# One 512-column v product per chunk for half of the heads, an in-place normalisation, and one distance tile for each large block

## The chip, the cores and the metric

The kernel is one program on one core of one Trainium2 chip. It is written in Bass with the Tile layer: the author writes operations on tiles, and a list scheduler fixes, before the kernel runs, the order of the instructions on each engine and the semaphores between them. The metric is the device time of one execution in microseconds (us). The kernel before takes 4754.6 us, the median of three runs (4753.3 to 4758.81).

The engines are TensorE (PE: matmuls; PEld: its weight loads), VectorE (DVE), ScalarE (ACT), GpSimd (POOL) and SyncE (SP), which issues nearly all DMAs. Everything is float32.

## The reference

Eight sequences of 512 tokens with 128 features pass through two blocks. The first is a causal attention with 16 heads of 8 features whose weights come from four Newton steps on lam, with weights 1/(lam - s). The second is a stack of six layers, each with a local attention (16 heads of 64 features, windows of 32 tokens) and a gated feed-forward part.

```python
x = x + attn(layernorm(x), Wqkv, Wo)            # first part: 16 heads of 8, Newton for lam
z = layernorm(x)
for i in range(6):                               # second part
    z = attn_layer(shift_tokens(z), Wqkv[i], q_scale[i], k_scale[i], Wo[i]) + z
    z = ffn_layer(shift_tokens(z), ln_g[i], ln_b[i], W1[i], b1[i], W2[i], b2[i]) + z
x = x + z

def attn_layer(x, Wqkv, qs, ksc, Wo):
    q, k, v = heads(x @ Wqkv)                    # 16 heads of 64
    q, k = rotary(l2norm(q) * qs), rotary(l2norm(k) * ksc)
    return local_attention(q, k, v) @ Wo         # each window of 32 sees itself and the one before
```

The change touches how v is made in `attn_layer`, and, in the first part, the layer norm and the tile that holds the distances lam - s of a block of queries.

## The kernel before

Two streams of work share the engines.

The first part (`streams`, L168 to L498) is a generator that is advanced in small steps. `project` (L203) loads one sequence into `xb`, `normalized_T` (L177) writes the normalised copy into a second tile `xn` on POOL (L189 to L194), PE transposes it, and ACT writes the transpose back (L199); q, k and v of the first part come from it. `evaluations` (L294) runs the Newton steps. For the two large blocks of queries, rb 3 and rb 2, it takes a distance tile `d` (L298) from a pool of two buffers, both as wide as block 3 needs (1856 columns), and block 2 uses the first 1344 of them. `enter` (L510) calls `normalized_T` again for the input of the second part.

The second part is a loop (L971 to L1045). A unit is one layer of one sequence; there are 48. A unit has four quarters of four heads, and a quarter has two pairs of heads, so a unit takes eight passes of the loop, and there are 384 passes. In each pass the program text asks, in this order, for: `turn` (L738, transposes of q and k, product tiles `ptq`, copies `qT`), `gather` (L790, the sums over the keys, from `v3`), `turn_weights` (L782, `pT`), `prepare_qk` of a half of a later quarter (L670: two products `m` of 512 columns, each multiplied by the tables on DVE at L683 and squared on ACT at L689, with two additions on POOL), `turn_sums` (L812: transposes `po` of L815 and the copy `oT`, L819), `weigh` (L752, 32 x 2 small score products `s`), `prepare_v` (L710), one step of the feed-forward part of the unit before (`further`, L943), and `leave` (L821: the output product `acc`, which reads `oT`). Between these, `tick` advances the first part. The first part has no steps left from about 3480 us on, and from there the passes are the second part alone.

A quarter is prepared over two passes: in each, `prepare_qk` and `prepare_v` treat two of the four chunks of 128 tokens. `prepare_v` makes, for the four heads of the quarter, one product of 256 columns for each of the two chunks; both go into one PSUM bank, and one ACT copy of 128x512 (L718) takes them to the staging tile `v`, of which there are three in rotation (L655, L668). A float32 product is issued to PE as two weight loads and two matmul instructions. After the second pass of a quarter `spread` (L723) issues 18 DMAs on SP that lay v out by windows in `v3`.

The feed-forward part of a unit begins in the pass after the unit's last one, and one of its steps stands in each pass between `prepare_v` and `leave`: its transposes, then the gate products `gp` (three), then the value products `ap` (three), then the products `y` (three).

Most product tiles of the second part come from one pool, `ps_a`, of three PSUM banks (`bank`, L646; its other branch is not reached with eight sequences, since `done_steps` ends at 29 x 72 and the branch asks for 33 x 72). A product has to wait until the last reader of its bank is done. In the passes looked at, the scheduler gave `prepare_v` the bank of the pass's first product `m`.

Of the kernel before, what the change touches and what calls it, by code (L numbers as in the profile page):

```python
# [9 lines left out]
F32 = mybir.dt.float32  # L10
# [6 lines left out]
P = 128  # L17
N = 512
NT = N // P
D = 128  # L20
# [9 lines left out]
DHL = 64  # L30
# [20 lines left out]
def tile_kernel(  # L51
# [18 lines left out]
    nc = tc.nc  # L70
# [22 lines left out]
    dp = ctx.enter_context(tc.tile_pool(name="dp", bufs=2))  # L93
    tr = ctx.enter_context(tc.tile_pool(name="tr", bufs=1))
    pj = ctx.enter_context(tc.tile_pool(name="pj", bufs=1))
# [72 lines left out]
    def streams(pools, bank1):  # L168

        ns_p, dp, tr, pj, sm = pools  # L170
# [6 lines left out]
        def normalized_T(xb, dst):  # L177
            st = sm.tile([P, NT, 6], F32, name="st")
            mv = sm.tile([P, NT, 2], F32, name="mv")
            for c in range(NT):  # L180
                nc.vector.bn_stats(st[:, c, :], xb[:, c, :])
                nc.vector.bn_aggr(mv[:, c, :], st[:, c, :])
                if c % 2:
                    yield
            rstd = sm.tile([P, NT], F32, name="rstd")
            nc.scalar.activation(rstd, mv[:, :, 1], AF.Ln, bias=eps_ln)
            nc.scalar.activation(rstd, rstd, AF.Exp, scale=-0.5)
            yield
            xn = pj.tile([P, NT, D], F32, name="xn", tag="xn")  # L189
            for c in range(NT):  # L190
                nc.gpsimd.tensor_scalar(
                    xn[:, c, :], xb[:, c, :], mv[:, c, 0:1], rstd[:, c : c + 1],
                    ALU.subtract, ALU.mult,
                )  # L194
                yield
            pt = bank1([P, N], "pt")
            for c in range(NT):
                nc.tensor.transpose(pt[:, c * P : (c + 1) * P], xn[:, c, :], ident)
            nc.scalar.copy(dst if dst is not None else xn.rearrange("p c d -> p (c d)"), pt)  # L199
            yield  # L200
            return xn.rearrange("p c d -> p (c d)")
# [30 lines left out]
        def keys(rb, a):  # L232
            return (rb + 1) * P - Q * (3 - a)

        def pieces(d, rb):
            at = [sum(keys(rb, c) for c in range(a)) for a in range(5)]
            return [d[:, at[a] : at[a + 1]] for a in range(4)]

        def width(rb):
            return sum(keys(rb, a) for a in range(4))  # L240
# [44 lines left out]
        def halves(d, rb):  # L285
            n = keys(rb, 0) + keys(rb, 1)
            return d[:, 0:n], d[:, n : width(rb)]

        def statistics(t, d, rb, a):
            nc.vector.bn_stats(  # L290
                t["st"][:, 4 * rb + a].rearrange("p u k -> p (u k)"), pieces(d, rb)[a]
            )

        def evaluations(t):  # L294

            late = []
            for rb in (3, 2):
                d = dp.tile([P, width(3)], F32, name="d")[:, 0 : width(rb)]  # L298
                for h in range(2):
                    for a in (2 * h, 2 * h + 1):  # L300
                        c = 4 * rb + a
                        nc.scalar.activation(  # L302
                            pieces(d, rb)[a], pieces(t["ns"][rb], rb)[a], AF.Ln,
                            bias=t["lam"][:, c : c + 1],
                        )
                    if late:
                        statistics(t, *late.pop(0))
                    yield
                    e = halves(d, rb)[h]
                    nc.scalar.activation(e, e, AF.Exp, scale=-1.0)  # L310
                    if late:
                        statistics(t, *late.pop(0))
                    yield
                    late += [(d, rb, 2 * h), (d, rb, 2 * h + 1)]
            for rb in (1, 0):
                d = t["df"][rb]
                nc.scalar.activation(d, d, AF.Ln)
                if late:
                    statistics(t, *late.pop(0))
                if rb:  # L320
                    yield
                nc.scalar.activation(d, d, AF.Exp, scale=-1.0)
                if late:
                    statistics(t, *late.pop(0))
                yield
                late += [(d, rb, a) for a in range(4)]
            for n in (3, 3, 2):
                for _ in range(n):
                    if late:
                        statistics(t, *late.pop(0))  # L330
                yield
# [87 lines left out]
        def stieltjes(seqs):  # L419
# [36 lines left out]
            def newton(now, k):  # L456
                if k == 0:
                    first_lam(now)
                    yield
                now["st"] = sm.tile([P, H, 2, 3], F32, name="stw")  # L460
                now["df"] = {}
                for rb in (1, 0):
                    now["df"][rb] = d = dp.tile([P, width(rb)], F32, name=f"df{rb}", bufs=1)
                    add_lam(now, d, rb)
                yield
                yield from evaluations(now)
                step(now)
                yield
# [107 lines left out]
    k2 = ctx.enter_context(tc.tile_pool(name="k2", bufs=1))  # L576
# [69 lines left out]
    def bank(shape, name):  # L646
        if done_steps >= (4 * NB + 1) * STEPS:
            turns["n"] += 1
            if turns["n"] % 5 > 2:
                return ps_1.tile(shape, F32, name=name, tag="p1")  # L650
        return ps_a.tile(shape, F32, name=name, tag="mm")

    PQ = 2
    HQ = 2 * PQ
    vst = [k2.tile([P, NT, 2, PQ, DHL + 1], F32, name=f"v{i}") for i in range(3)]  # L655
    for v in vst:
        nc.gpsimd.memset(v.rearrange("p c e h d -> p (c e h) d")[:, :, DHL:], 1.0)

    guarded = [k2.tile([P, 2, 2 * HQ, 2], F32, name=f"raw{i}") for i in range(3)]
    for raw in guarded:  # L660
# [4 lines left out]
    def begin(u, qt, xs):  # L665
        qn = qp.tile([P, NT, 2, HQ, DHL], F32, name="qn")
        v3 = vp.tile([P, NQ, PQ, DHL + 1], F32, name="v3")
        return dict(u=u, qt=qt, xs=xs, qn=qn, v3=v3, v=vst[len(groups) % 3])  # L668

    def prepare_qk(g, wqkv, tab, cs):  # L670
        xs, q0 = g["xs"], (g["qt"] % 2) * HQ * DHL
# [36 lines left out]
            )  # L708

    def prepare_v(g, wqkv, cs):  # L710
        xs, q0 = g["xs"], (g["qt"] % 2) * PQ * DHL
        pv = bank([P, 2, 2, PQ * DHL], "pv2")
        cols = wqkv[:, 2, :].rearrange("i (e f) -> i e f", e=2)[:, :, q0 : q0 + PQ * DHL]
        for i, c in enumerate(cs):
            nc.tensor.matmul(  # L715
                pv[:, i], lhsT=xs[:, c * P : (c + 1) * P], rhs=cols, start=True, stop=True,
            )
        nc.scalar.copy(  # L718
            g["v"][:, cs[0] : cs[0] + 2].rearrange("p c e h d -> p (c e h) d")[:, :, 0:DHL],
            pv.rearrange("p c e (h d) -> p (c e h) d", d=DHL),  # L720
        )

    def spread(g):  # L723
        v3 = g["v3"].rearrange("p n h d -> p n (h d)")
        vc = g["v"].rearrange("p c e h d -> p c e (h d)")
        for e in range(2):
            at = slice(e * KB, e * KB + WIN)
            for u in range(UB):
                own = vc[u * QB : (u + 1) * QB, :, e]
                c = 1 if u == 0 else 0  # L730
                nc.sync.dma_start(v3[e * KB + WIN : (e + 1) * KB, u + c * UB :: UB, :], own[:, c:])
                if u < UB - 1:
                    nc.sync.dma_start(v3[at, u + 1 :: UB, :], own)
                else:
                    nc.sync.dma_start(v3[at, UB::UB, :], own[:, 0 : NT - 1])
            nc.sync.dma_start(v3[e * KB : (e + 1) * KB, 0, :], vc[0:KB, 0, e])
# [183 lines left out]
    groups = []  # L920
# [25 lines left out]
    def open_quarter(i):  # L946
        u, qt = quarters[i]
        if qt == 0 and units[u][0] == 0:
            settle()
        groups.append(begin(u, qt, shifted(units[u][1], ep) if qt == 0 else groups[-1]["xs"]))  # L950

    def prepared(g):
        u, qt = g["u"], g["qt"]
        spread(g)
        if u + 1 < len(units) and units[u + 1][0] != units[u][0]:
            if qt % 2:
                wq[qt // 2] = load_qkv(units[u + 1][0], qt // 2)
# [4 lines left out]
    for h in range(2):  # L962
        cs = (2 * h, 2 * h + 1)
        prepare_qk(groups[0], wq[0], tab[h], cs)
        prepare_v(groups[0], wq[0], cs)
# [5 lines left out]
    while t < slots + LAG + 1 or parts:  # L971
        i, p = t // PQ, t % PQ
# [21 lines left out]
        i, h = (t + 1) // PQ + 1, (t + 1) % PQ  # L994
        if i < len(quarters):
# [3 lines left out]
            cs = (2 * h, 2 * h + 1)  # L999
            prepare_qk(ahead, wq[ahead["qt"] // 2], tab[h], cs)  # L1000
            u = ahead["u"] + 1
# [19 lines left out]
        if ahead:  # L1021
            prepare_v(ahead, wq[ahead["qt"] // 2], cs)
            if h == PQ - 1:
                prepared(ahead)
# [3 lines left out]
        if last:  # L1028
            u, qt = last["g"]["u"], last["g"]["qt"]
# [13 lines left out]
        u = (t + 6) // NS  # L1043
# [53 lines left out]
```

## Time and profile before

| what | value |
| --- | --- |
| median of three runs | 4754.6 us (4753.3 to 4758.81) |
| the profiled execution's own time | 4761.87 us |
| its span, first to last instruction | 4760.2 us |
| mean granted TensorE clock | 0.936 of full speed |
| PE idle of the span | 661 us (4760.2 - 4099.0) |
| products of `prepare_v` (L715) | 1536 instructions, 451.0 us busy |
| copies of `prepare_v` (L718) | 384, 224.0 us busy |

The profiled execution took 7.3 us more than the median of the runs. A row of the page gives line, engine, operation, the tiles written and read, shape, count, then the busy time of the group, the mean time of one instruction in ns, and the idle time before them with what ended it. The count of PE instructions is twice the number of products, because a float32 product is two instructions. Busy time of overlapping instructions is counted once, so a matmul's mean duration (415 ns for a v instruction) is more than its share of the busy time (451.0 / 1536 = 294 ns).

### The profile page before, as it was taken

What the parts mean: (1) busy time and instruction counts of PE and PEld (TensorE: products, weight loads), DVE (VectorE), ACT (ScalarE), POOL (GpSimd) and SP (SyncE); (2) the same over time, 40 slices, a digit from 0 to 9 for tenths busy, and PEclk for the clock granted to TensorE, in tenths of its full rate; (3) what the DMA queues carried; (4) which work ended last, traced back from release to release, by engine and by line L of the source; (5) the groups of instructions that cost most, each with busy time, mean ns of one, the idle gap of its engine ahead of it and who ended that gap; (6) DMA issues with size and microseconds to landing.
All of it is one profiled execution on the core that took longest, in us unless ns stands there. A gap on an engine that the chain in (4) does not pass through costs nothing.

```text
span 4760.2 us, 165854 instructions
## 1 busy us (share of the span) xinstructions
PE 4099.0 (86%) x68749; PEld 2520.1 (53%) x68749; DVE 3940.5 (83%) x8788; ACT 3538.8 (74%) x6717; POOL 3174.8 (67%) x4081
## 2 busy tenths in 40 slices
PE   4345688888889898789999989998999999999998
PEld 1222455555545555455555555555666666666665
DVE  7878788888888888889998999998777777777775
ACT  6998677877778778777888888888666666666664
POOL 4453666666666667676777777677677777777774
PEclk7666799999999999899999999999999999999999
DMA  1000222222222222132222222222333333333332
GB/s 48 1 1 1 64 60 53 66 61 62 60 53 65 55 70 55 37 71 59 63 53 59 64 48 70 54 57 66 72 88 84 80 87 72 87 76 85 87 73 59
DMA packets 558912, 288.87 MB, mean 61 GB/s; under 512 B 97580, under 2 KB 541264, under 8 KB 558160
## 3 DMA queue, kind: packets, MB, share of 16 engines
q1 hardware_dynamic: 558160, 278.26, 25.1%
q8 instruction: 543, 8.90, 0.8%
q14 instruction: 209, 1.71, 0.1%
HBM read 66.21 MB, written 7.34 MB: 15 GB/s over the span
## 4 chain that ended last, share of the span: by engine, by line
PE 41%; ACT 26%; DVE 20%; POOL 7%; issue 3%; SPq 1%; DMA 1%; ACTq 0%; POOLq 0%; DVEq 0%
PE m L678 8%; ACT d L302 7%; ACT d L310 5%; DVE qr L683 5%; PE ptq L744 5%; PE pv L715 4%; PE po L798 4%; PE acc L823 4%; DVE stw L290 3%; PE pT L787 3%; PE s L763 3%; ACT sq L689 2%; DVE raw L700 2%; PE s L264 2%; POOL ns L277 2%
## 5 line engine op out<-in xcount | busy, mean ns | idle before, releaser
L693 POOL TENSOR_TENSOR qn<-qr 128x512 f32<-128x512 f32 x768 | 968.9, 1278 | 561.4 <-DVE qr L683 524.0
L683 DVE TENSOR_TENSOR qr<-m,tab 128x1024 f32<-128x1024 f32 x768 | 912.8, 1217 | 197.3 <-PE m L678 168.6
L706 POOL TENSOR_TENSOR qn<-qn,ss 128x512 f32<-128x512 f32 x768 | 785.0, 1043 | 259.7 <-ACT ss L703 251.7
L678 PE MATMUL m<-wqkv,xs 128*128 128x512 f32 x1536 | 773.9, 618 | 45.8 <-ACT qT L749 39.0
L689 ACT ACTIVATE sq<-m 128x512 f32<-128x512 f32 x768 | 459.0, 600 | 394.2 <-DVE qr L683 382.7
L302 ACT ACTIVATE d<-ns,lam 128x416 f32<-128x416 f32 (+7 forms) x1024 | 590.3, 625 | 101.9 <-DVE lam L346 83.4
L290 DVE BATCH_NORM_STATS2 stw<-d 128x6 f32<-128x480 f32 (+7 forms) x1024 | 545.0, 563 | 104.2 <-ACT d L310 101.6
L277 POOL TENSOR_TENSOR df<-ns,lam 128x160 f32<-128x160 f32 (+7 forms) x1024 | 398.4, 425 | 308.8 <-DVE sw L344 152.0
L774 POOL TENSOR_TENSOR pr<-pr,nm 128x512 f32<-128x512 f32 x384 | 400.0, 1042 | 260.7 <-DVE ss L701 160.5
L749 ACT COPY qT<-ptq 128x512 f32<-128x512 f32 x768 | 430.4, 586 | 173.9 <-PE ptq L744 172.5
L700 DVE TENSOR_REDUCE raw<-sq 128x16 f32<-128x1024 f32 x384 | 466.6, 1215 | 47.8 <-ACT sq L689 36.2
L715 PE MATMUL pv<-wqkv,xs 128*128 128x256 f32 x1536 | 451.0, 415 | 56.5 <-ACT sq L689 48.9
L744 PEld LDWEIGHTS ptq<-ident,qn 128*128 128x128 f32 x3072 | 368.3, 144 | 214.0 <-issue 118.7
L744 PE MATMUL ptq<-ident,qn 128*128 128x128 f32 x3072 | 439.3, 281 | 12.6 <-ACT v L718 5.6
L365 PE MATMUL dTp<-ident,ns 128*128 128x128 f32 x1280 | 242.0, 306 | 232.4 <-POOL ns L277 100.6
L310 ACT ACTIVATE d<-d 128x864 f32<-128x864 f32 (+3 forms) x512 | 440.4, 870 | 0.0
L823 PE MATMUL acc<-oT,wo 128*128 128x512 f32 x768 | 407.4, 612 | 15.2 <-ACT oT L819 14.8
L678 PEld LDWEIGHTS m<-wqkv,xs 128*128 128x128 f32 x1536 | 261.8, 196 | 249.0 <-issue 140.3
L798 PE MATMUL po<-v,prT 64*32 64x65 f32 x24576 | 372.5, 227 | 10.6 <-DVE pr L768 10.2
L264 PE MATMUL s<-kn,qj 32*32 32x288 f32 (+14 forms) x4096 | 331.8, 415 | 35.3 <-DVE mn L268 29.9
L798 PEld LDWEIGHTS po<-v,prT 64*32 64x32 f32 x24576 | 284.8, 106 | 142.1 <-issue 70.2
L763 PE MATMUL s<-qT,qT 64*32 64x64 f32 x24576 | 355.3, 226 | 1.6 <-DVE o L807 1.6
(138 smaller groups left out, 8016.1 us busy)
## 6 DMA issues: line engine op xcount, KB each, us to landing
v<-v SPq DMA_DIRECT2D x2304, 65.0 KB
v<-v SPq DMA_DIRECT2D x768, 48.8 KB
wqkv<-in_L_ffn_Wqkv_dram SPq DMA_DIRECT2D x72, 256.0 KB
v<-v SPq DMA_DIRECT2D x384, 32.5 KB
wqkv<-in_L_ffn_Wqkv_dram SPq DMA_DIRECT2D x72, 128.0 KB
wo<-in_L_ffn_Wo_dram SPq DMA_DIRECT2D x36, 256.0 KB
tab<-tabs SPq DMA_DIRECT2D x36, 256.0 KB
w<-in_L_ffn_W_dram SPq DMA_DIRECT2D x18, 341.0 KB
```

Source lines behind the costliest of these rows:

```text
L290: nc.vector.bn_stats(t["st"][:, 4 * rb + a].rearrange("p u k -> p (u k)"), pieces(d, rb)[a])
L302: nc.scalar.activation(pieces(d, rb)[a], pieces(t["ns"][rb], rb)[a], AF.Ln, bias=t["lam"][:, c : c + 1],)
L310: nc.scalar.activation(e, e, AF.Exp, scale=-1.0)
L678: nc.tensor.matmul(m.rearrange("p t h e -> p t (h e)"), lhsT=xs[:, c * P : (c + 1) * P], rhs=wqkv[:, 0:2, q0 : q0 + HQ * DHL], start=True, ...
L683: nc.vector.tensor_tensor(qr, m.unsqueeze(1).to_broadcast([P, 2, 2, HQ, DHL]), tab[:, i].rearrange("p (k t) e -> p k t e", k=2).unsqueeze( ...
L693: nc.gpsimd.tensor_tensor(g["qn"][:, c].rearrange("p t h (u e) -> p (t h) u e", u=2), halves_of[:, 0], halves_of[:, 1, :, ::-1, :], ALU.add,)
L700: nc.vector.tensor_reduce(raw[:, :, :, 0], sq, axis=AX.X, op=ALU.add)
L706: nc.gpsimd.tensor_tensor(qc, qc, ss[:, i, :].unsqueeze(2).to_broadcast([P, 2 * HQ, DHL]), ALU.mult)
L715: nc.tensor.matmul(pv[:, i], lhsT=xs[:, c * P : (c + 1) * P], rhs=cols, start=True, stop=True,)
L744: nc.tensor.transpose(pt[:, c * P : (c + 1) * P], g["qn"][:, c, t, 2 * p : 2 * p + 2, :].rearrange("p h e -> p (h e)"), ident,)
L798: nc.tensor.matmul(po[u * QB : (u + 1) * QB, e, c, :], lhsT=prT[rows, c, u * QB : (u + 1) * QB], rhs=g["v3"][rows, n, p, :], start=True, s ...
L823: nc.tensor.matmul(acc, lhsT=wo[:, pp % (NPAIR // 2), :], rhs=a["oT"], start=(pp == 0), stop=(pp == NPAIR - 1),)
```

## The change

`prepare_v` works only when the quarter is the first of a half of the heads (an even quarter), and then for both quarters of the half: one product of 512 columns for each chunk, each in a bank of its own, and one copy of 128x512 after each. For an odd quarter it does nothing. The staging tile holds two quarters, and there are two of them in place of three; `spread` still runs once for each quarter and reads the quarter's part. The number of copies (384) and of DMAs is what it was; the number of products is halved, from 768 of 256 columns to 384 of 512.

In the scheduled order of the changed program, a pass that prepares an even quarter has `s`, two `pv` products, the feed-forward step if there is one, `acc`; a pass that prepares an odd quarter has `s`, the feed-forward step, `acc`. Of the eight passes of a unit, four in two runs of two have no v products. In the last stage, the feed-forward steps that stand between `s` and `acc` there are: none in one of the four, the transposes `px` in the second, `gp` in the third, `ap` in the fourth.

The staging tiles take 4160 bytes of each partition more than before (2 x 8320 in place of 3 x 4160). The two other edits give 2048 bytes each: the normalised input of the first part overwrites `xb` and `xn` is no longer a tile of its own, and block 2 has its own, narrower distance tile. The pool of `d` had two buffers, used in turn by block 3 and block 2; now each block has one tile.

```diff
-            xn = pj.tile([P, NT, D], F32, name="xn", tag="xn")
+            xn = xb
...
-                d = dp.tile([P, width(3)], F32, name="d")[:, 0 : width(rb)]
+                d = dp.tile([P, width(rb)], F32, name=f"d{rb}", bufs=1)
...
-    vst = [k2.tile([P, NT, 2, PQ, DHL + 1], F32, name=f"v{i}") for i in range(3)]
+    vst = [k2.tile([P, NT, 2, 2, PQ, DHL + 1], F32, name=f"v{i}") for i in range(2)]
...
-        return dict(u=u, qt=qt, xs=xs, qn=qn, v3=v3, v=vst[len(groups) % 3])
+        return dict(u=u, qt=qt, xs=xs, qn=qn, v3=v3, v=vst[len(groups) // 2 % 2])
...
     def prepare_v(g, wqkv, cs):
-        xs, q0 = g["xs"], (g["qt"] % 2) * PQ * DHL
-        pv = bank([P, 2, 2, PQ * DHL], "pv2")
-        cols = wqkv[:, 2, :].rearrange("i (e f) -> i e f", e=2)[:, :, q0 : q0 + PQ * DHL]
-        for i, c in enumerate(cs):
+        if g["qt"] % 2:
+            return
+        cols = wqkv[:, 2, :].rearrange("i (e q f) -> i q e f", e=2, q=2)
+        for c in cs:
+            pv = bank([P, 2, 2, PQ * DHL], "pv2")
             nc.tensor.matmul(
-                pv[:, i], lhsT=xs[:, c * P : (c + 1) * P], rhs=cols, start=True, stop=True,
-            )
-        nc.scalar.copy(
-            g["v"][:, cs[0] : cs[0] + 2].rearrange("p c e h d -> p (c e h) d")[:, :, 0:DHL],
-            pv.rearrange("p c e (h d) -> p (c e h) d", d=DHL),
-        )
+                pv, lhsT=g["xs"][:, c * P : (c + 1) * P], rhs=cols, start=True, stop=True
+            )
+            nc.scalar.copy(
+                g["v"][:, c].rearrange("p q e h d -> p (q e h) d")[:, :, 0:DHL],
+                pv.rearrange("p q e (h d) -> p (q e h) d", d=DHL),
+            )
...
-        vc = g["v"].rearrange("p c e h d -> p c e (h d)")
+        vc = g["v"][:, :, g["qt"] % 2].rearrange("p c e h d -> p c e (h d)")
```

More of the change, by code (lines that the diff above doesn't have):

```diff
@@ L654, in tile_kernel @@
     HQ = 2 * PQ
-    vst = [k2.tile([P, NT, 2, PQ, DHL + 1], F32, name=f"v{i}") for i in range(3)]
+    vst = [k2.tile([P, NT, 2, 2, PQ, DHL + 1], F32, name=f"v{i}") for i in range(2)]
     for v in vst:
-        nc.gpsimd.memset(v.rearrange("p c e h d -> p (c e h) d")[:, :, DHL:], 1.0)
+        nc.gpsimd.memset(v.rearrange("p c q e h d -> p (c q e h) d")[:, :, DHL:], 1.0)
     guarded = [k2.tile([P, 2, 2 * HQ, 2], F32, name=f"raw{i}") for i in range(3)]
```

## The prediction

> **What bounds the kernel now.** I read the engine shares and the chain of waits on the page, then busy time by stretches, then the groups by line, and last the timeline of one pass in the stage without first-part work.
>
> ```profile
> PE 4099.0 (86%) x68749; PEld 2520.1 (53%) x68749; DVE 3940.5 (83%) x8788; ACT 3538.8 (74%) x6717; POOL 3174.8 (67%) x4081
> ...
> PE 41%; ACT 26%; DVE 20%; POOL 7%; issue 3%; SPq 1%; DMA 1%; ACTq 0%; POOLq 0%; DVEq 0%
> ```
>
> PE is the fullest engine, but holds only 41% of the chain. The stretches say where (time; then PE, PEld, DVE, ACT and POOL busy; granted clock; DMA share; GB/s):
>
> ```profile
> 600.00:3480.00 2880.00, 2563.23 (x42308) 1534.96 (x42309) 2506.84 (x5750) 2255.92 (x4286) 1976.36 (x2569) 0.96 0.26 60
> 3480.00:4600.00 1120.00, 1098.79 (x20749) 724.80 (x20736) 869.32 (x1319) 706.04 (x1438) 826.68 (x828) 1.00 0.36 81
> ```
>
> From 600 to 3480 us ("middle") PE is busy 89%, DVE 87%, ACT 78%: they bind in turns. After it ("tail") PE is busy 98%, no other engine over 78%. The same stretches for L715 alone count 924 and 528 instructions, four to a pass: 231 passes in the middle, 132 in 1120 us of the tail, so 8.5 us a tail pass.
>
> ```profile
> L678 PE MATMUL m<-wqkv,xs 128*128 128x512 f32 x1536 | 773.9, 618 | 45.8 <-ACT qT L749 39.0 <-POOL xs L640 4.0 <-ACT sq L689 1.3
> L715 PE MATMUL pv<-wqkv,xs 128*128 128x256 f32 x1536 | 451.0, 415 | 56.5 <-ACT sq L689 48.9 <-ACT oT L819 5.3 <-DVE pr L768 1.6
> L718 ACT COPY v<-pv 128x512 f32<-128x512 f32 x384 | 224.0, 583 | 41.5 <-PE pv L715 40.3
> ```
>
> The m row is the price of a 512-column instruction with the same kind of weights; L718 already copies 128x512. One tail pass (start, length):
>
> ```profile
> 4001.58 1.88 PE L678 MATMUL m<-wqkv,xs 128*128 128x512 f32 x4
> ...
> 4003.30 0.60 PE L815 MATMUL po<-ident,o 128*128 128x128 f32 x4
> ...
> 4003.83 0.86 PE L763 MATMUL s<-qT,qT 64*32 64x64 f32 x64
> ...
> 4003.97 0.60 ACT L689 ACTIVATE sq<-m 128x512 f32<-128x512 f32 x1 [1.61 <-DVE qr L683]
> ...
> 4004.47 0.58 ACT L819 COPY oT<-po 128x512 f32<-128x512 f32 x1
> 4004.62 0.73 PEld L715 LDWEIGHTS pv<-wqkv,xs 128*128 128x128 f32 x4
> 4004.62 1.13 PE L715 MATMUL pv<-wqkv,xs 128*128 128x256 f32 x4
> ...
> 4005.10 0.60 ACT L689 ACTIVATE sq<-m 128x512 f32<-128x512 f32 x1
> ...
> 4005.59 1.02 PE L823 MATMUL acc<-oT,wo 128*128 128x512 f32 x2
> ...
> 4006.11 0.58 ACT L718 COPY v<-pv 128x512 f32<-128x512 f32 x1
> ```
>
> The reader is to see two things. PE runs without a gap, and pv takes 5.59 - 4.62 = 0.97 us of it. And pv is a cover: acc needs oT, whose copy ends at 4004.47 + 0.58 = 4005.05, 0.43 us after s gives PE free. oT is late because it stands on ACT behind the square, which waits for DVE's product with the tables.
>
> **PE's work, before any wait.** Four m instructions take 4003.30 - 4001.58 = 1.72 us start to start, 0.43 each. Four of 256 columns take 0.97, 0.243 each, more than half: their weight loads alone are busy 0.73. A pass that makes v will issue four of 512, 1.72 us, +0.75; one that makes none saves 0.97. Over two passes that is -0.22, over 384 passes 192 x 0.22 = 42 us: 25 in the middle (231 passes), 17 in the tail (153). By busy time it would be 451.0 - 768 x (773.9 / 1536) = 64 us; I take 42, because the distances include the weight loads that hold PE up.
>
> The Trainium skill ("TensorE: Matmul & The Clock Gate", Back-to-back issue gap) gives for streams of weight load and matmul some 81 ns at 128 columns and 131 at 512, so by estimate 98 at 256. By its ratio, 1.34, a pass with v would take 1.30 us and the whole would save 384 x 0.97 - 192 x 1.30 = 123 us; the rows above have a ratio of 1.77, and the sum goes by the rows.
>
> **The tail, pass by pass.** The first v product still takes the first m's bank (square done 4004.57), the second in the changed order takes oT's bank (done 4005.05, wanted at 4.62 + 0.86 = 4005.48): no wait. The next products, ptq and pT, wait for the two copies, on ACT behind the exponentials until 4006.21, so done at 6.8 and 7.4; they are wanted at about 7.7 and 9.1. So four passes a unit pay 0.75: +3.00.
>
> The four passes without v, by what stands between s and acc: (1) nothing: acc waits for oT until about 4005.10, so 0.49 of 0.97 comes back. (2) Four transposes px, 0.44 start to start, cover the wait: acc at 5.10 for 5.59 + 0.44, 0.92 back. (3) Three products gp hold all three banks, so the next ptq waits for DVE's gate operations, which begin (4044.23, against s at 4040.51) 3.72 after s and take 0.69 each; today it uses pv's bank instead. Moved to 4003.83 the two ptq start near 8.3 and 9.0; m then comes at about 10.85, against 4047.95 - 36.68 = 11.27: 0.42 back. (4) Three products ap: today the third waits 0.66 for a gate operation, and the qT copies stand on ACT behind v's copy (4056.92). With neither, m is let go by qT's copy at about 11.4 after moving by 46.37, against 4059.00 - 46.37 = 12.63: 1.2 back. Together -3.03, so -0.03 a unit, and over 19 units -1 us, rounded. Of the tail's 17 us almost nothing is left.
>
> **The middle.** There pv holds 2.4% of the chain (700 to 3450 us), 66 us, of some 221 x 1.06 = 234 us that its products take at the lower clock: 28%. The same share of 25 us is -7 us. Bounds: -25, if each freed time is used, and +30, if passes without v give back 0.49 and those with v pay 0.75 (115 pairs x 0.26). I take -7, since first-part products can fill the gap before acc there.
>
> **ACT and SP.** Copies stay 384 of 0.583. The wait for the staging tile's old DMAs stands before one copy in four in place of each: the build has 391 event semaphores fewer on ACT, 38 ns the longest kind before L718, 15 us of its queue at most; nine of that in the middle, by ACT's 26% of the chain -2 (bounds 0 and -9). An even quarter's copy must wait for the spread of three quarters before, as now; behind that first copy stand the second copy, the qT copies and so m. The spread is issued in 18 x 0.65 = 11.7 us from two and a half passes earlier, so some 20 us cover it; uncovered it would cost up to 5 us an even quarter. SP's order and number of DMAs stay.
>
> **The small edits: 0.** xb is now free after PE's reads and ACT's copy, not after POOL's normalisation. The next load into it comes passes later, except for the second sequence entering at the start: four transposes and a copy, up to +2 us once. Block 3 and block 2 used the two buffers of d by turns, so one tile each makes no new wait; only the block that had it before can be waited for.
>
> **Sum.** -1 - 7 - 2 + 0 = -10 us: the profiled 4761.9 becomes 4751.9, and the median of 4754.6, 7.3 lower, 4744.6. I put it at 4744.
>
> **The rivals.**
> Full saving: the passes without v lose no time and the 42 us all arrive, 4713. For it: 98% of PE in the tail. Against: acc's own wait for oT, 38.7 us already at L823, and bank waits at ap.
> The cover gone (slower): in the passes without v, acc waits for oT, or the ptq behind gp and ap for their gates, and only 0.49 returns in all four, while four pay 0.75: 4 x 0.26 x 19 = +20 us in the tail, 4775, and up to 4805 with the middle's +30. It decides as soon as a pass without v returns less than 0.75 on the mean; my mean is 0.76, so this is close.
> Nothing: the new order of the list scheduler moves waits in the middle by as much as the 10 us, 4755. For it: the order differs on every engine, and DVE at 87% and ACT at 78% of the middle do the same work.
>
> **How the numbers follow.** 0.2% of 4754.6 is 9.5 us, about what a measurement can tell from no change. Small gain 0.40 (4730 to 4750, of this 0.05 within 0.2%), full saving 0.11, the cover gone 0.30, nothing 0.19. So faster 0.46, same 0.24, slower 0.30. The range 4716 to 4776 leaves out the last of the full saving and the slower end of the cover gone.
>
> **What would show it.** L715's successor has 768 instructions of 128x512 and near 387 us busy. In the tail acc starts about 1.3 us after s in a bare pass without v, on oT; pv takes 1.72 in the others; a unit of eight passes keeps its 67.1 us (today between the additions to xT at L1039, 4007.55 and 4074.67). If a tail unit takes under 66.3 us the full saving is right, over 68 us the cover gone. I am wrong most simply if the second v product or the ptq after it waits for ACT in the middle.

## The result and the profile after

The changed kernel takes 4789.2 us (median of four runs, 4780.76 to 4794.63) against 4756.7 us for the kernel before in the same comparison: a ratio of 1.0065, 95% interval 1.0053 to 1.0078. The forecast was 4744 us and a small gain; it is a loss of 32 us, outside the range of 4716 to 4776. The two profiled executions below differ by 25 us, since that of the kernel before took 5 us more than its median here and that of the changed one 2 us less.

The page of the changed kernel has these lines for the ones shown of before:

```profile
span 4785.1 us, 163872 instructions
...
PE 4115.5 (86%) x67981; PEld 2362.9 (49%) x67981; DVE 3939.3 (82%) x8788; ACT 3555.0 (74%) x6717; POOL 3173.9 (66%) x4080
...
PE 39%; ACT 20%; DVE 19%; POOL 6%; issue 2%; SPq 1%; DMA 1%; ACTq 0%; DVEq 0%; POOLq 0%
```

The reader is to see that PE issues 768 matmul instructions fewer and is busy for 16.5 us more. The view of one line says what PE waited for ahead of it (us, times; weight loads and matmuls together). Of the v products, L716 of the changed kernel, the longest are these:

```profile
  ACT sq L689: 79.6, 116
  issue: 48.0, 183
  ACT oT L820: 34.2, 105
```

Before, they waited 112.2 us for the squares and 14.0 for oT: the two together have not grown. The same view of `acc`, first of the kernel before and then of the changed one:

```profile
  issue: 58.6, 213
  ACT oT L819: 38.7, 63
```

```profile
  issue: 97.1, 361
  ACT oT L820: 84.8, 119
```

The waits of acc for oT have more than doubled. This view counts the idle time of weight loads and of matmuls, which can run side by side; the rows of the pages have the matmuls alone, two of the kernel before and then three of the changed one:

```profile
L744 PE MATMUL ptq<-ident,qn 128*128 128x128 f32 x3072 | 439.3, 281 | 12.6 <-ACT v L718 5.6
L823 PE MATMUL acc<-oT,wo 128*128 128x512 f32 x768 | 407.4, 612 | 15.2 <-ACT oT L819 14.8
...
L745 PE MATMUL ptq<-ident,qn 128*128 128x128 f32 x3072 | 448.3, 283 | 39.8 <-DVE gate L887 17.3
L824 PE MATMUL acc<-oT,wo 128*128 128x512 f32 x768 | 416.0, 624 | 34.6 <-ACT oT L820 34.0
L716 PE MATMUL pv<-wqkv,xs 128*128 128x512 f32 x768 | 401.3, 637 | 31.3 <-ACT sq L689 26.0
```

PE's idle time ahead of acc grew by 19 us and ahead of ptq by 27, and ahead of pv it fell by 25 (from 56.5). To place the loss in time I use one event of each unit, the addition of the finished acc to xT (L1039 before, L1040 after), numbered 0 to 47. All times are us of the two profiled executions:

| stretch | before | after | difference |
| --- | --- | --- | --- |
| start to unit 0 | 664.3 | 657.6 | -6.7 |
| unit 0 to unit 29 (the middle) | 2865.2 | 2882.2 | +17.0 |
| unit 29 to unit 47 (the tail) | 1203.0 | 1217.7 | +14.7 |
| unit 47 to the end | 27.6 | 27.5 | -0.1 |
| span | 4760.2 | 4785.1 | +24.9 |

The middle of the two executions, PE alone (time; busy; granted clock; DMA share; GB/s), before and after:

```profile
664.30:3529.50 2865.20, 2556.43 (x42148) 0.96 0.26 60
657.60:3539.80 2882.20, 2571.46 (x41665) 0.96 0.25 60
```

PE is idle for 2865.2 - 2556.4 = 308.8 us of the middle before and for 2882.2 - 2571.5 = 310.7 after. The longer waits of acc and ptq there are made up by shorter ones elsewhere; what grew, by 15 us, is PE's busy time, and the mean granted clock, to three digits, fell from 0.962 to 0.958 of full speed. In the tail the clock is 1.00 in both, and busy time grew by 7.0 us and idle time by 7.7.

In the tail each pass can be read from the start of one pair of products m to the next. One unit of each kernel:

| what stands between s and acc | before | after | difference | predicted |
| --- | --- | --- | --- | --- |
| nothing (no v after) | 7.12 | 6.73 | -0.39 | -0.49 |
| px (no v after) | 7.67 | 6.76 | -0.91 | -0.92 |
| v | 7.12 | 7.99 | +0.87 | +0.75 |
| v, pn | 7.65 | 8.41 | +0.76 | +0.75 |
| gp (no v after) | 9.69 | 9.49 | -0.20 | -0.42 |
| ap (no v after) | 11.05 | 10.06 | -0.99 | -1.2 |
| v, y | 9.70 | 10.55 | +0.85 | +0.75 |
| v | 7.12 | 8.06 | +0.94 | +0.75 |
| unit | 67.12 | 68.05 | +0.93 | -0.03 |

Two of those passes in the timeline of the changed kernel (PE alone; start, length), a bare one and one with v:

```profile
4026.15 0.86 PE L764 MATMUL s<-qT,qT 64*32 64x64 f32 x64
4027.42 1.13 PE L824 MATMUL acc<-oT,wo 128*128 128x512 f32 x2 [0.41 <-ACT oT L820]
4028.38 1.04 PE L745 MATMUL ptq<-ident,qn 128*128 128x128 f32 x8
...
4039.63 0.86 PE L764 MATMUL s<-qT,qT 64*32 64x64 f32 x64
4040.45 1.98 PE L716 MATMUL pv<-wqkv,xs 128*128 128x512 f32 x4
4042.27 1.02 PE L824 MATMUL acc<-oT,wo 128*128 128x512 f32 x2
```

In the bare pass acc waits for oT and starts 1.27 us after s, as foreseen. In the pass with v, the products take 4042.27 - 4040.45 = 1.82 us, not 1.72; and in the bare pass acc itself takes 4028.38 - 4027.42 = 0.96 us where it takes 0.86 behind v products. The first product of 256 or 512 columns behind s pays 0.10 us more than the next ones, whichever it is (the three gp behind s take 2.68 us, behind v products 2.57). Where px with its 128 columns is the first, it pays 0.06, and acc behind it takes 0.95. Before, the first was nearly always a v product.

### The profile page after: what moved, and what is told of

The parts are those of the page before. It is cut to its first block, busy times and chain, and to the rows that moved or that the text cites. A ratio compares the mean times of both kernels' runs of the same rounds, so it can differ in the third digit from the quotient of the medians.

```text
span 4785.1 us, 163872 instructions
## 1 busy us (share of the span) xinstructions
PE 4115.5 (86%) x67981; PEld 2362.9 (49%) x67981; DVE 3939.3 (82%) x8788; ACT 3555.0 (74%) x6717; POOL 3173.9 (66%) x4080
## 4 chain that ended last, share of the span: by engine, by line
PE 39%; ACT 20%; DVE 19%; POOL 6%; issue 2%; SPq 1%; DMA 1%; ACTq 0%; DVEq 0%; POOLq 0%
PE m L678 8%; DVE qr L683 5%; ACT d L302 5%; PE ptq L745 5%; PE pv L716 4%; PE po L799 4%; PE acc L824 4%; ACT d L310 3%; ACT sq L689 3%; PE pT L788 3%; DVE stw L290 2%; DVE raw L700 2%; PE s L764 2%; PE gp L873 2%; POOL ns L277 2%
## 5 line engine op out<-in xcount | busy, mean ns | idle before, releaser
L750 ACT COPY qT<-ptq 128x512 f32<-128x512 f32 x768 | 419.8, 587 | 186.2 <-PE ptq L745 182.4
L716 PE MATMUL pv<-wqkv,xs 128*128 128x512 f32 x768 | 401.3, 637 | 31.3 <-ACT sq L689 26.0
L799 PE MATMUL po<-v,prT 64*32 64x65 f32 x24576 | 379.8, 227 | 14.7 <-DVE pr L769 14.4
L264 PE MATMUL s<-kn,qj 32*32 32x288 f32 (+14 forms) x4096 | 334.7, 414 | 32.2 <-DVE mn L268 27.5
```

The costliest lines, as they stand in the source:

```text
L716: nc.tensor.matmul(pv, lhsT=g["xs"][:, c * P : (c + 1) * P], rhs=cols, start=True, stop=True)
L799: nc.tensor.matmul(po[u * QB : (u + 1) * QB, e, c, :], lhsT=prT[rows, c, u * QB : (u + 1) * QB], rhs=g["v3"][rows, n, p, :], start=True, s ...
```

## The experiments

### The small edits alone

```diff
-            xn = pj.tile([P, NT, D], F32, name="xn", tag="xn")
+            xn = xb
...
-                d = dp.tile([P, width(3)], F32, name="d")[:, 0 : width(rb)]
+                d = dp.tile([P, width(rb)], F32, name=f"d{rb}", bufs=1)
```

This is the kernel before with these two edits and the old v.

> The kernel before with only the two small edits (input normalised in place, one distance tile for each large block); v is made as before. Theory U (the uneven passes cost the time: v work gathered in half of the passes, no cover for oT in the others): these edits cost nothing, 4757 us within 10. Rival L (the small edits, or the new order and addresses that any edit brings, cost it): 4770 to 4790 us, and the middle stage longer by some 20 us with every pass as full as before.

Measured: 4752.1 us against 4753.3, ratio 1.000 (0.9991 to 1.0009). The two edits cost nothing, and neither does the new order that came with them; the loss comes with the new way of making v. Its profile has 2855.4 us from unit 0 to unit 29, where the kernel before has 2865.2: single profiles of equal work differ by 10 us in the middle. The v change without the two edits was not run.

### The same uneven passes with products of 256 columns

```diff
-            nc.tensor.matmul(
-                pv, lhsT=g["xs"][:, c * P : (c + 1) * P], rhs=cols, start=True, stop=True
-            )
+            for q in range(2):
+                nc.tensor.matmul(
+                    pv[:, q], lhsT=g["xs"][:, c * P : (c + 1) * P], rhs=cols[:, q],
+                    start=True, stop=True,
+                )
```

> The changed kernel with each 512-column v product split into two of 256 columns into the same bank; passes with and without v as in the change. Theory U: as slow as the change, 4789 us within 8, and four products of 256 with one start take about 1.82 us in a pass of the last stage, as the two of 512 do now. Rival S (256 columns are dearer per column, held up by weight loads, as the prediction had it): 8 x 0.243 = 1.94 us a pass, and 192 x 0.12 = 23 us more than the change, 4812 us.

Measured: 4799.9 us, ratio to the kernel before 1.0106 (1.009 to 1.0121); that is 11 us over the change, between the two expectations and within neither. The timeline of a pass decides for the reason behind the first:

```profile
4097.26 1.99 PE L717 MATMUL pv<-wqkv,xs 128*128 128x256 f32 x8
4099.09 1.02 PE L826 MATMUL acc<-oT,wo 128*128 128x512 f32 x2
```

Eight instructions of 256 columns take 1.83 us, four of 512 take 1.82. Width saves nothing on PE in a pass of the tail. The units of the tail are as long as in the change (1219.9 us from unit 29 to unit 47 against 1217.7); the 11 us are in the middle (2893.6 against 2882.2), near the spread just seen between profiles of equal work. The medians of the runs differ by more than their noise, and why is open.

### Each v product of the kernel before issued twice

```diff
-            nc.tensor.matmul(
-                pv[:, i], lhsT=xs[:, c * P : (c + 1) * P], rhs=cols, start=True, stop=True,
-            )
+            for _ in range(2):
+                nc.tensor.matmul(
+                    pv[:, i], lhsT=xs[:, c * P : (c + 1) * P], rhs=cols, start=True, stop=True,
+                )
```

> The kernel before with each 256-column v product issued twice into the same place (output unchanged): four more instructions in each pass, with no start of their own. If the 0.97 us of a pass is a start of 0.10 and four times 0.2175, a pass of the last stage grows by 0.87 us and a unit of eight by 7.0 (67.1 to 74.1 us). If weight loads hold a 256-column instruction at 0.243, a pass grows by 0.97 and a unit by 7.8 (to 74.9 us). The whole grows by 200 to 330 us.

Measured: 4941.3 us, +188 us, ratio 1.0394 (1.038 to 1.0408). The whole grew less than expected, the pass by what the first reading says:

```profile
4117.81 1.99 PE L716 MATMUL pv<-wqkv,xs 128*128 128x256 f32 x8
4119.64 1.02 PE L824 MATMUL acc<-oT,wo 128*128 128x512 f32 x2
```

Four instructions took 0.97 us and eight take 1.83: 0.86 for four more, so 0.215 each and 0.11 for the start. A unit of the tail goes from 67.1 to about 73.5 us, 0.5 less than 8 x 0.86 would make it; the wait of the third ap product, 0.66 us once a unit before, is gone. The second number is the price of PE's work in the middle: 2949.9 - 2865.2 = 85 us for 29 units of 6.88 us, 42% of it. The mean granted clock of the middle is 0.977 in this run and 0.962 before, so a part of that low price is a faster clock.

### acc moved behind the next transposes

```diff
+        if gone:
...
+            leave(gone, wo[hv], acc)
...
         tick(1)
...
-        if last:
...
-            leave(last, wo[hv], acc)
...
+        gone = last
```

The block around `leave` stands, word for word, behind `turn` of the next pass. On the changed kernel:

> The changed kernel with the output product acc moved behind the next pass's transposes of q and k, so that it no longer stands where oT is late. Theory U: the bare pass without v gets its wait back (about 0.4 us, once in eight passes of the last stage) and the middle loses the 57 us that acc and its weight load wait for oT; 4765 to 4780 us. Rival L: acc's wait is only where time is lost, not why, and the wait moves to ptq; 4789 us within 8.

Measured: 4767.1 us, ratio to the kernel before 1.0028 (1.0017 to 1.0038); 22 us below the change. Against the kernel before of the same runs (4753.3) the loss is 14 us in place of 32. The waits of acc, same view as above:

```profile
  issue: 35.7, 128
  ACT oT L820: 11.6, 17
```

The wait for oT falls from 84.8 to 11.6 us, the middle from 2882.2 to 2866.0, the tail from 1217.7 to 1211.3. In the middle this is not less idle time of PE: 2866.0 - 2553.4 = 312.6 us, as much as in the change, with longer waits now ahead of ptq (38.9 us in place of 23.8) and of the transposes po of L816 (55.4 in place of 45.2). Its busy time fell by 18 us, and the granted clock there is 0.962 again:

```profile
661.40:3527.40 2866.00, 2553.41 (x41675) 0.96 0.25 60
```

The bare pass of the tail now takes 6.28 us:

```profile
4076.56 1.88 PE L678 MATMUL m<-wqkv,xs 128*128 128x512 f32 x4
...
4078.81 0.93 PE L764 MATMUL s<-qT,qT 64*32 64x64 f32 x64
4079.67 1.09 PE L745 MATMUL ptq<-ident,qn 128*128 128x128 f32 x8
4080.60 1.02 PE L824 MATMUL acc<-oT,wo 128*128 128x512 f32 x2
4081.55 0.86 PE L799 MATMUL po<-v,prT 64*32 64x65 f32 x64
...
4082.84 1.88 PE L678 MATMUL m<-wqkv,xs 128*128 128x512 f32 x4
```

That is 0.84 below the 7.12 of before, nearly the whole 0.97 - 0.10. So theory U names the tail's wait rightly; its wait of the middle moved to ptq and po, as rival L has it, and yet the time came back. The control, the same move on the kernel before:

> The kernel before with acc moved behind the next pass's transposes of q and k, the control to the same edit on the changed kernel. Theory U: with v products in every pass oT is nearly always ready (38.7 us of waits at acc against 84.8 in the change), so the move gains at most 8 us: 4745 to 4757 us. Rival L (moving acc is good by itself, whatever v does): as large a gain as on the changed kernel, 22 us, 4731 us.

Measured: 4766.7 us against 4755.0, ratio 1.0023 (1.0015 to 1.0032). Where every pass has v products, moving acc is a loss, not even the small gain expected; its profile, of an execution 9 us faster than the median, puts the loss in the tail (1213.5 against 1203.0: the px, pn and gp passes take 7.90, 7.90 and 10.00 us in place of 7.67, 7.65 and 9.69), none in the middle (2855.9). So the gain on the changed kernel undoes something that the change did, and is not a gain of the move by itself. In the tail that is the wait of the bare pass; in the middle it is open.

### Five banks in the last stage

```diff
-        if done_steps >= (4 * NB + 1) * STEPS:
+        if done_steps >= total:
```

The branch that lets the second part use the first part's two PSUM banks is never reached in either kernel, because `total` counts seven sequences in this stream and the condition eight. With it mended, on the kernel before:

> The kernel before, with the second branch of bank() reached once the first part is done, so that the last stage has five PSUM banks in place of three. Theory U with bank waits: only the third ap product waited for a bank (0.66 us in one pass of eight), so a unit of the last stage goes from 67.1 to about 66.4 us and the whole gains 10 to 14 us, 4740 us. Rival (PE is the bound and banks do not matter): 4754 us within 5.

Measured: 4725.5 us against 4755.0, ratio 0.9935 (0.9921 to 0.9948), more than twice the gain expected. The ap pass before and with five banks:

```profile
4051.96 1.88 PE L883 MATMUL ap<-xn_ffn,w 128*128 128x512 f32 x4
4053.67 1.02 PE L823 MATMUL acc<-oT,wo 128*128 128x512 f32 x2
4054.62 0.42 PE L798 MATMUL po<-v,prT 64*32 64x65 f32 x20
4055.70 1.09 PE L883 MATMUL ap<-xn_ffn,w 128*85 128x512 f32 x2 [0.66 <-DVE gate L886]
```

```profile
4035.90 2.74 PE L883 MATMUL ap<-xn_ffn,w 128*128 128x512 f32 x6
4038.48 1.02 PE L823 MATMUL acc<-oT,wo 128*128 128x512 f32 x2
4039.34 1.04 PE L744 MATMUL ptq<-ident,qn 128*128 128x128 f32 x8
```

The pass falls from 11.05 to 9.69 us, as long as the gp pass: not only the 0.66 but also the interruption of the work around it goes. A unit takes 65.7 us, and the units at the turn of a layer, 68.0 to 71.0 before, now take 65.6 to 66.8. On the changed kernel:

> The changed kernel with five PSUM banks in the last stage. Theory U: the ptq products behind gp and ap no longer wait for gate operations; those two passes give back up to 0.6 and 0.7 us more, a unit goes from 68.0 to about 66.8 us, and the whole from 4789 to about 4767 us. Only the bare pass still waits for oT. Rival (the last stage loses by the price of the 512-column products alone): a unit stays at 68.0 us, 4789 us.

Measured: 4764.3 us, ratio to the kernel before 1.0015 (1.0006 to 1.0024): 25 us better than the change, and 9 us over the kernel before in place of 32. A unit takes 66.8 us, as expected, and the ptq products behind gp follow acc at once:

```profile
4049.96 2.84 PE L873 MATMUL gp<-xn_ffn,w 128*128 128x512 f32 x6
4052.64 1.02 PE L824 MATMUL acc<-oT,wo 128*128 128x512 f32 x2
4053.50 1.04 PE L745 MATMUL ptq<-ident,qn 128*128 128x128 f32 x8
```

In the middle nothing changes (2882.7 us). With both repairs on the changed kernel:

> The changed kernel with both repairs, acc later and five banks in the last stage. Theory U: the two waits are separate and the gains add: 4767 less some 15 us, 4752 us, level with the kernel before, since the products themselves save almost nothing (1.82 us in half of the passes and a start of 0.10 in the others, against 0.97 in each: 4 us of 42). If the products did save 42 us, this would show it: 4715 us.

Measured: 4742.7 us against 4755.0, ratio 0.9974 (0.9964 to 0.9984). The two repairs add: each against the kernel before of its own runs, they gain 19 and 23 us, and both together 45. That is 10 us more than expected, since five banks are worth more. It beats the kernel before, but not the kernel before with the same banks: 4725.5 us is the fastest of all, and it makes v in the old way. With both waits repaired the change is still 17 us behind that.

## Why the prediction was wrong, point by point

**PE's work, the step that failed first.** The prediction had "four of 256 columns take 0.97, 0.243 each, more than half: their weight loads alone are busy 0.73", and from it 42 us of PE work saved. The runs show 0.215 us for an instruction of 256 columns and 0.43 for one of 512, and 0.10 to 0.11 once, for the first product behind s. So the weight loads did not hold up every instruction. The 0.10 itself may be one: the first v product's weight load starts with its matmul, at 4004.62 in the lines of before, where that of acc starts 0.21 ahead of its matmul.

```profile
4005.38 0.41 PEld L823 LDWEIGHTS acc<-oT,wo 128*128 128x128 f32 x2
```

No run separates this from a price of leaving the small products of s. In the changed kernel the 0.10 is paid in every pass, by v where there is v and by px, gp, ap or acc where there is none. So, at the tail's prices, the work is 384 x 0.97 = 372.5 us before and 192 x 1.82 + 192 x 0.10 = 368.6 after: 4 us are saved in place of 42. The row of m could not show it, since m comes behind other large products. The estimate by the ratio of 1.34 from the Trainium skill ("TensorE: Matmul & The Clock Gate", Back-to-back issue gap) was further off: float32 products here have 0.43 / 0.215 = 2.0.

**The tail.** The passes with v were mis-sized by the same 0.10 (3.42 us a unit in place of 3.00). In the passes without v most of the mechanisms were right: acc waits for oT until 1.27 us after s; px covers that wait; ptq waits for the gate operations behind gp. The wait behind ap was missed: the prediction had it gone, and ptq waits there 0.66 us for a gate operation in place of the third ap product:

```profile
4071.03 0.66 PE L745 MATMUL ptq<-ident,qn 128*128 128x128 f32 x4 [0.66 <-DVE gate L887]
```

The four passes returned 2.49 in place of 3.03: the bare pass 0.10 less, since acc now pays the start, and the gp and ap passes 0.2 each, of which 0.10 is the start that gp and ap now pay. A mean return of 0.62 us is below the 0.75 that the rival named as its point, and below the 0.85 that a pass with v really costs.

**The middle.** The prediction took "the same share of 25 us is -7 us" and let first-part products "fill the gap before acc there". The 25 us did not exist, so there was nothing to take a share of, and the middle got 17 us longer in single profiles. The gap before acc did grow, from 13.7 to 22.5 us of PE's idle time there, but the whole idle time is 308.8 us before and 310.7 after: it is PE's busy time that grew, by 15 us. The granted clock of the middle was lower, 0.958 against 0.962; if PE's busy time went with it, that would be some 10 of the 15 us (an estimate: 2556.4 x 0.962 / 0.958 - 2556.4). The whole runs go the same way: their mean clocks are 0.9338 for the change with five banks (11 runs), 0.9365 with acc moved as well (8) and 0.9364 for the kernel before beside them (24). Moving acc took 16 us of the middle back and the clock with it; whether the lower clock makes the loss, and why the uneven passes have it, was not tested. So the term of -7 is the second that failed, +17 in its place, and how the middle loses it stays open. The bound of +30 covers the size, but it was added up from waits, and the idle time does not show them.

**Copies, semaphores, DMAs, small edits.** The small edits cost nothing, as said. No v copy was seen to wait for the staging tile's DMAs. The count of event semaphores at the v copies fell from 760 to 380, and no gain can be seen beside the loss.

**The rivals.** The cover gone is what happened in the tail: 4775 us with the tail alone and 4805 with the middle were its two ends, and the kernel takes 4789. It had 0.30. For the middle its mechanism is not shown, so that 4789 lies between its ends is in part luck. The choice between it and the small gain was made on a mean return of 0.76 against 0.75, with a bias of 0.10 in both numbers that pulled them apart. The full saving is excluded by the price of an instruction, which is the same for each column at both widths, and by the kernel with both repairs, which still trails the old v products with five banks.

**Still open.** After both repairs 17 us remain against the kernel before with five banks: 15 of them in the tail by the profiles (1185.7 against 1170.7 us). There the four passes with v pay 0.85 to 0.86 each, and the bare, px and gp passes return 0.86 to 0.91, but the ap pass only 0.18 (9.51 against 9.69 us), since it waits 0.61 us for the exponentials. That makes 0.55 us a unit, some 10 of the 15 us; the rest was not traced. Open too is how the middle of the changed kernel loses its time.

## What to carry to other kernels

A stretch of instructions in a timeline is a start plus a slope. Its mean is no price for a change of width: take the slope from two lengths, and ask who pays the start when the stretch is taken away.

Work on the fullest engine may be the cover of a wait that stands right behind it. Gathering such work into every second pass saves nothing if the amount is the same, and opens the wait in the passes that are left empty; look for what the next instruction needs and when that is ready, and price the full and the empty pass each for itself. A wait that has grown is not yet lost time: sum the engine's idle time over the stretch, and look at its busy time and clock, before the wait is called the cause.

When a wait for a buffer shows up, check that the buffers the program means to use are in use. A condition that is never true cost this kernel 0.65%.

## What the hardware showed beyond what was expected

A float32 product's instructions cost 0.215 us for 256 columns and 0.43 us for 512 in a stream at a granted clock of 1.00, so a column costs the same at both widths. The first product with 128 x 128 weights behind a run with 64 x 32 costs 0.10 us more if it has 256 or 512 columns, and 0.06 more if it has 128. The last one ahead of such a run costs 0.09 us more: with acc moved ahead of the other run of small products, acc takes 4081.55 - 4080.60 = 0.95 us in place of 0.86. Whether the change of tile shape or an uncovered weight load is the reason was not tested.

A microsecond of PE work, added where PE is busy 89% and DVE 87%, costs 0.42 us; added where PE is busy 98%, 0.82 us (1304.0 - 1203.0 = 101 us for 18 units of 6.88 us). The first figure holds a change of the clock, from 0.962 to 0.977 of full speed in that stretch.
